# A Taylor attention layer and six windowed-attention layers in one kernel: head norms from a quarter of the array with roots by way of DRAM, queries packed for two groups, the final norm in three places

## The chip, the cores and the metric

The kernel runs on one core of a Trainium2 chip. The metric is the device time of one execution in microseconds (us). A core has five engines that run side by side, each with its own queue of instructions taken in order: TensorE (PE in the profile; its weight loads are listed apart as PEld), VectorE (DVE), ScalarE (ACT), GpSimd (POOL) and SyncE (SP), which here only issues DMAs. An instruction waits at the head of its engine's queue until the semaphores that it needs are set, and everything behind it on that engine waits too.

## The reference

Eight sequences (B = 8) of 512 tokens (N) with 128 features go through two residual blocks. The first is an attention whose weights are a second-order Taylor polynomial of the scores, with a root-mean-square norm of every head's output:

```python
q, k = heads of 16 features;  v = heads of 64           # 16 heads
A = tril(1 + s + s*s/2),  s = q . k / 4                 # qf . kf of taylor_exp
y = A @ v
y = y * rsqrt(mean(y*y over the 64) + 1e-5) * g_weight
out = y @ Wo.T
x = x + layernorm(out)                                  # of layernorm(x) as the input
```

The second block is a stack of six layers, each a local attention in windows of 32 with rotary tables and a gated feed-forward part:

```python
for i in range(6):
    x = attn_layer(shift_tokens(x), ...) + x
    x = ffn_layer(shift_tokens(x), ...) + x
x = x_before + layernorm(x)
```

All is in float32.

## The kernel before

**Two stages.** In the first, the Taylor attention runs over 8 sequences times 4 groups of 4 heads: 32 groups (G = 4b + g). In the second, the six layers run over 6 x 8 x 4 units of 128 tokens (t = 0 to 191), as one software pipeline in which the steps of a unit are spread over later units (`at(t, lag, step)`). The order of TensorE's instructions is the order of the program (`manual_schedule` for PE). On the other engines a scheduler sets the order ahead of time, from priorities and its own idea of durations; `high_priority` and `issue_behind` steer it.

**Tiles.** Pools hand out tiles by tag, and a tag has one to three buffers. A new tile of a tag waits until the last readers of the tile that held its buffer are done. PSUM has four tags: `mm` (2 buffers of 2 banks), `tr` (2 of 1 bank), and `s` (1 of 2 banks). Tags are shared between the stages, so that `t2`, for one, holds roots of head norms in the first stage and half of the turned q and k in the second.

**The first stage** is a list of slots, three to a group: `slot(k)` with k = 3G + ph. In a slot, `squares(k)` multiplies k and q of the group in four row tiles of 32 rows (L261) for the blocks of 128 keys in `STEPS`, ScalarE squares the sums (L270), and VectorE adds one and applies the triangle to the diagonal block (L274). Two slots later `weigh` multiplies with v in two column tiles of 64 columns (L291) into y (PSUM tag `s`, one buffer). After a group's last step, in the next group's slot ph 1, VectorE copies y out with the sums of earlier blocks added (yT, L299, high priority) and ScalarE squares it (ysq, L304). `head_norm(G - 2)` stands in slot ph 0 of every group. It multiplies the squares with a 128x128 block matrix of ones (`same`), so that every feature's row receives its head's sum (L312, two matmuls over 512 columns, two passes each in float32), takes Ln (L313) and Exp (L315) on ScalarE for the roots, and multiplies y by gain and root on VectorE (L317). Between them, `project_qk` (L230, L231) makes q and k of the next group in ph 1, `project_v` (L239, L243) its v in ph 2.

For each sequence, `attn_out(b - 1)` stands in group 1's slot ph 2 of the next sequence: 32 output matmuls over the four groups of the sequence (L327), a layer norm (L335), the residual on GpSimd (L336), a store of 256 KB to DRAM (L337, `x1`) and a second layer norm (L340). `to_state(b - 1)` transposes that into the stack's state three slots later. The next sequence's input is loaded (L145), normed (L200) and transposed (`in_by_features`) in groups 0 and 1.

After the last slot the second stage begins; its unit t = 0 holds `head_norm(31)`, its unit t = 1 `attn_out(7)`.

**The second stage**, for one unit: `proj` (L430, then L438, L446, L454, and L461 on GpSimd), `values` (L488), `sum_squares`, `unit_length` (L474, L477 on GpSimd), `by_features` (transposes, L69), `scores` (L551, maxima L559, exponentials L563), `by_keys`, `weigh_values` (L592), `out_by_features`, `out_project` (L621); for a whole sequence, every fourth unit, `feed_norm`, `feed_first`, `feed_middle` (L646, L648) and `feed_last` (L681). In the units with gelus (every fourth), ScalarE loads the Gelu table and then the table of Ln and Exp again. In the last layer, nine units behind, `out_by_tokens` transposes the result (L699) and `store` norms it (L709: statistics L106 and L108, root L95 and L97, L118 on VectorE), adds the residual on GpSimd (L712) and stores it (L713). Both stand in a unit with gelus.

**At the start**, SyncE issues the first weights (`tw[:, 0]`), the first input, and the other weights in that order.

Of the kernel before, what the change touches and what calls it, by code (L numbers as in the profile page):

```python
# [8 lines left out]
F32 = mybir.dt.float32  # L9
# [19 lines left out]
def sandwich_kernel(ctx: ExitStack, tc: tile.TileContext, ins: dict, out: bass.AP):  # L29
# [20 lines left out]

    dram = ctx.enter_context(tc.tile_pool(name="dram", bufs=1, space=bass.MemoryType.DRAM))
    x1 = [dram.tile([P, NB, DM], F32, tag=f"x1_{b}", name=f"x1_{b}") for b in range(B)]
    state = [const.tile([P, N + 1], F32, tag=f"state_{b}", name=f"state_{b}") for b in range(B)]
    for b in range(B):
        nc.vector.memset(state[b][HD:P, 0:1], 0.0)
# [37 lines left out]
    def inverse_root(dst, src, bias=0.0):  # L93

        ln = nc.scalar.activation(dst, src, AF.Ln, bias=bias)  # L95
        issue_behind(ln, tables[-1])
        exps.append(nc.scalar.activation(dst, dst, AF.Exp, scale=-0.5))  # L97

    def layer_norm(pool, dst, src, nb, by_log=False, later=False):


        st = pool.tile([P, nb, 6], F32, tag="ln_st", name="ln_st")
        mv = pool.tile([P, nb, 2], F32, tag="ln_mv", name="ln_mv")
        rs = pool.tile([P, nb], F32, tag="ln_rs", name="ln_rs")
        for j in range(nb):
            nc.vector.bn_stats(st[:, j, :], src[:, j, :])  # L106
        for j in range(nb):
            nc.vector.bn_aggr(mv[:, j, :], st[:, j, :])  # L108
        if by_log:
            inverse_root(rs, mv[:, :, 1], eps)  # L110
        else:
            nc.vector.tensor_scalar(rs, mv[:, :, 1], EPS, None, ALU.add)
            nc.scalar.activation(rs, rs, AF.Sqrt)
            nc.vector.reciprocal(rs, rs)

        def last(behind=None):
            for j in range(nb):
                t = nc.vector.tensor_scalar(  # L118
                    dst[:, j, :], src[:, j, :], mv[:, j, 0:1], rs[:, j : j + 1], ALU.subtract, ALU.mult
                )  # L120
                if behind is not None:
                    issue_behind(t, behind)

        if later:
            return last
        last()
# [4 lines left out]
    f2 = ctx.enter_context(tc.tile_pool(name="f2", bufs=2))  # L131
    f3 = ctx.enter_context(tc.tile_pool(name="f3", bufs=3))
    f1 = ctx.enter_context(tc.tile_pool(name="f1", bufs=1))

    HF = HD // 2
    NP = H // 2
# [30 lines left out]
    nc.vector.memset(same, 0.0)  # L167
# [56 lines left out]

    def project_qk(G):
        b, g = divmod(G, NQ)
        gr[G]["qk"] = qk = f2.tile([P, 2, N], F32, tag="pe", name=f"tqk_{G}")
        for s in range(2):
            ps = psum.tile([P, N], F32, tag="tr", name="qk")
            nc.tensor.matmul(ps, wqk[:, s, g * P : (g + 1) * P], bt[b]["xlT"], start=True, stop=True)  # L230
            nc.scalar.copy(qk[:, s], ps)  # L231

    def project_v(G):
        b, g = divmod(G, NQ)
# [16 lines left out]
    def squares(k):  # L251

        G, s = steps[k]
        qk = gr[G]["qk"]
        sc = [psum.tile([P, 2, N], F32, tag="mm", name="sc") for _ in range(2)]
        at_, places = 0, []
        for m in STEPS[s]:
            n = N - m * P
            for h in range(4):
                r = slice(32 * h, 32 * h + 32)  # L260
                nc.tensor.matmul(  # L261
                    sc[h // 2][:, h % 2, at_ : at_ + n],
                    qk[r, 1, m * P : (m + 1) * P], qk[r, 0, m * P :], start=True, stop=True,
                    skip_group_check=True,
                )
            places.append((m, at_, n))
            at_ += n
        am = f2.tile([P, 4, 512], F32, tag=("qk", "v2")[k % 2], name="am")
        for i in range(2):
            nc.scalar.activation(  # L270
                am[:, 2 * i : 2 * i + 2, :at_], sc[i][:, :, :at_], AF.Square, bias=1.0, scale=0.25
            )
        for m, o, n in places:
            nc.vector.scalar_tensor_tensor(  # L274
                am[:, :, o : o + P], am[:, :, o : o + P], 1.0,
                keep.unsqueeze(1).to_broadcast([P, 4, P]), ALU.add, ALU.mult,
            )
        gr[G]["am", s] = am, places

    def weigh(k):  # L280
# [12 lines left out]
                    start=(m == 0), stop=(m == NB - 1), skip_group_check=True,  # L293
                )
        if s == len(STEPS) - 1:
            yT = f2.tile([P, 2, NB, P], F32, tag="sq", name="yT")
            with tc.high_priority():
                for i in range(2):
                    nc.vector.tensor_tensor(  # L299
                        yT[:, i], y[:, i].rearrange("p (n m) -> p n m", m=P),  # L300
                        bt[b]["vs"][:, 2 * g + i, :].unsqueeze(2).to_broadcast([P, NB, P]), ALU.add,
                    )
            ysq = f2.tile([P, 2, N], F32, tag="t1", name="ysq")
            nc.scalar.activation(ysq, yT.rearrange("p a n m -> p a (n m)"), AF.Square)  # L304
            gr[G]["yT"], gr[G]["ysq"] = yT, ysq

    def head_norm(G):
        yT, ysq = gr[G].pop("yT"), gr[G].pop("ysq")
        rs = f2.tile([P, 2, N], F32, tag="t2", name="rs")
        for i in range(2):  # L310
            ps = psum.tile([P, N], F32, tag="tr", name="ms")
            nc.tensor.matmul(ps, same, ysq[:, i], start=True, stop=True)  # L312
            ln = nc.scalar.activation(rs[:, i], ps, AF.Ln, bias=eps4, scale=1.0 / HD)  # L313
            issue_behind(ln, tables[-1])
        exps.append(nc.scalar.activation(rs, rs, AF.Exp, scale=-0.5))  # L315
        gr[G]["yn"] = yn = f1.tile([P, 2, N], F32, tag=("qT", "pT", "on", "oT")[G % NQ], name="yn")
        nc.vector.scalar_tensor_tensor(  # L317
            yn.rearrange("p a n -> p (a n)"), yT.rearrange("p a n m -> p (a n m)"), gw,
            rs.rearrange("p a n -> p (a n)"), ALU.mult, ALU.mult,
        )  # L320

    def attn_out(b):

# [28 lines left out]
    def slot(k):  # L352
# [2 lines left out]
        b, g = divmod(G, NQ)  # L355
        if k < len(steps):
            squares(k)
        if ph == 0 and 0 <= G - 2 < NG:
            head_norm(G - 2)
        if ph == 1 and G + 1 < NG:  # L360
            project_qk(G + 1)
        if ph == 2 and G + 1 < NG:
# [4 lines left out]
            in_by_features(b + 1)  # L367
        if g == 1 and ph == 1 and b + 1 < B:
            sums_before(b + 1)
        if g == 1 and ph == 2 and b >= 1 and k < len(steps):  # L370
            attn_out(b - 1)
        if g == 2 and ph == 2 and b >= 1 and k < len(steps):
            to_state(b - 1)
        if 0 <= k - 2 < len(steps):
            weigh(k - 2)
# [326 lines left out]
            u["out"] = fo = f1.tile([P, NB, DM], F32, tag="fo", name="fo")  # L702
            nc.scalar.copy(fo, ps)

    def store(u):

        b, src = u["b"], u["out"]
        fo = src if b < B - 1 else f1.tile([P, NB, DM], F32, tag="fo", name="fo")
        layer_norm(f2, fo, src, NB, by_log=True)  # L709
# [19 lines left out]
    with tc.manual_schedule(engines={mybir.EngineType.PE}):  # L729
# [8 lines left out]
        for t in range(len(units) + 7):  # L738
# [49 lines left out]
            at(t, 1, scores)  # L788
            if t == len(units) + 5:
                at(t, 6, out_by_tokens)  # L790
                at(t, 6, store)
            at(t, 3, feed_normed, ends=True)
            at(t, 2, out_by_features)

# [37 lines left out]

def _attn_weights(given):

    import numpy as np

    parts = []
    for nm in ("Wq", "Wk"):
        w = given[f"L0_attn_{nm}"].reshape(H, FD, DM)
        parts.append(np.pad(w, ((0, 0), (0, FD), (0, 0))).reshape(2 * FD * H, DM).T)  # L840
    parts.append(given["L0_attn_Wv"].T)
    parts.append(given["L0_attn_Wo"].T.reshape(H // 2, P, DM).transpose(1, 0, 2).reshape(P, H // 2 * DM))
    return np.ascontiguousarray(np.concatenate(parts, 1))


# [39 lines left out]
```

## Time and profile before

| what | value |
|---|---|
| median of three runs | 3693.85 us (3693.65 to 3706.11) |
| the profiled execution | 3691.65 us |
| its span | 3689.8 us |
| granted TensorE clock, mean | 0.995 |
| first matmul of the first slot to the last y matmul of the first stage | 17.94 to about 532.24 us |
| six sequences' periods in the first stage, from L327 to L327 | 65.61, 67.25, 65.67, 65.67, 67.25, 62.03 us |
| four units in the fifth layer and at the start of the sixth | 64.35 us |
| four units with a store | 67.14 to 67.23 us |

The span runs from the first to the last instruction that the profiler shows. The granted clock is 0.97 in every third slice of 50 us and 1.00 in the others, which is where the periods of 67.25 us lie. Times of float32 matmuls come in pairs of passes: an instruction of the program is two instructions in the profile. Neighbouring matmuls overlap a little, so that what one step takes on TensorE is read from its start to the start of the next step, and is a little less than the duration beside it.

### The profile page before, as it was taken

The numbers are of one execution on the slowest core, as the hardware profiler recorded it, in microseconds if no ns is written. First come the engines' busy times: TensorE is split into PE (matmuls) and PEld (weight loads), VectorE is DVE, ScalarE is ACT, GpSimd is POOL, SyncE is SP. The second block draws the span as 40 slices with busy tenths as digits, with TensorE's granted clock in tenths as the row PEclk, the third lists the DMA queues.
The fourth block names the chain that finished last, engine by engine and source line by source line (L and its number), as shares of the span: only waits on it lengthen the run. The fifth ranks groups of instructions, "written<-read, shape, count | busy, mean of one in ns | idle before, by whom it ended". The sixth has DMA issues, their size and how long they took to land.

```text
span 3689.8 us, 152840 instructions
## 1 busy us (share of the span) xinstructions
PE 3632.2 (98%) x65216; PEld 2421.6 (66%) x65216; DVE 2808.2 (76%) x3915; ACT 2825.4 (77%) x6944; POOL 1844.7 (50%) x1311
## 2 busy tenths in 40 slices
PE   8999999999999999999999999999999999999997
PEld 4555556666676766667676666767666766766665
DVE  4555557788787878788787878878887887888885
ACT  5565557878787888888788888878888887877875
POOL 0000016555565555656555656656555565655552
PEclk9999999999999999999999999999999999999998
DMA  3000003222232222322222322222322222222221
GB/s 85 18 10 7 12 18 92 68 61 69 66 93 66 68 67 66 83 76 70 63 66 66 92 74 60 69 67 78 78 71 68 60 68 68 67 66 71 70 74 43
DMA packets 153220, 233.67 MB, mean 63 GB/s; under 512 B 32622, under 2 KB 53356, under 8 KB 151788
## 3 DMA queue, kind: packets, MB, share of 16 engines
q1 hardware_dynamic: 152556, 223.89, 23.7%
q8 instruction: 530, 8.68, 1.0%
q14 instruction: 134, 1.10, 0.1%
HBM read 24.54 MB, written 4.19 MB: 8 GB/s over the span
## 4 chain that ended last, share of the span: by engine, by line
PE 90%; ACT 8%; DVE 1%; issue 1%; POOL 0%; DMA 0%; POOLq 0%; DVEq 0%; SPq 0%; ACTq 0%
PE tr L69 19%; PE mm L430 14%; PE py L621 9%; PE mm L488 9%; PE po L592 8%; PE sp L551 6%; PE y L291 4%; ACT pe L563 4%; PE mm L646 4%; PE mm L648 3%; PE py L681 3%; PE sc L261 3%; PE vv L239 2%; PE po L327 1%; PE qk L230 1%; ACT L75 1%
## 5 line engine op out<-in xcount | busy, mean ns | idle before, releaser
L461 POOL TENSOR_TENSOR qk<-t,t 128x1024 f32<-128x1024 f32 x384 | 910.6, 2372 | 622.7 <-DVE t L446 414.6
L477 POOL TENSOR_TENSOR qk<-qk,ss 128x1024 f32<-128x1024 f32 x384 | 723.2, 1905 | 16.0
L430 PE MATMUL mm<-wqkv,state 128*128 128x512 f32 x1536 | 700.2, 596 | 2.6 <-ACT v L493 2.6
L563 ACT ACTIVATE pe<-sp,mx 128x64 f32<-128x64 f32 x3072 | 654.3, 381 | 7.6 <-DVE mx L559 7.6
L438 DVE TENSOR_TENSOR t<-mm,tab 128x1024 f32<-128x1024 f32 x384 | 468.2, 1219 | 217.5 <-PE mm L430 214.5
L454 ACT ACTIVATE sq<-mm 128x512 f32<-128x512 f32 x768 | 420.2, 603 | 126.9 <-DVE t L446 124.5
L446 DVE TENSOR_TENSOR t<-mm,tab 128x1024 f32<-128x1024 f32 x384 | 468.2, 1219 | 7.3 <-POOL qk L461 1.4
L430 PEld LDWEIGHTS mm<-wqkv,state 128*128 128x128 f32 x1536 | 273.0, 190 | 292.0 <-issue 240.9
L464 DVE TENSOR_REDUCE ss<-sq 128x16 f32<-128x1024 f32 x384 | 448.7, 1209 | 0.1
L69 PE MATMUL tr<-ident,qk 128*128 128x128 f32 x3072 | 441.8, 277 | 1.8 <-POOL qk L461 0.8
L69 PEld LDWEIGHTS tr<-ident,qk 128*128 128x128 f32 x3072 | 351.7, 141 | 120.1 <-issue 56.1
L621 PE MATMUL py<-oT,wo 128*128 128x128 f32 x3072 | 377.3, 276 | 0.3 <-ACT oT L614 0.3
L621 PEld LDWEIGHTS py<-oT,wo 128*128 128x128 f32 x3072 | 367.6, 195 | 0.5 <-ACT oT L614 0.5
L488 PE MATMUL mm<-wqkv,state 128*128 128x512 f32 x768 | 361.5, 593 | 0.2 <-ACT sq L454 0.2
L614 ACT COPY oT<-tr 128x512 f32<-128x512 f32 x384 | 205.5, 587 | 168.3 <-PE tr L69 165.7
L551 PEld LDWEIGHTS sp<-kT,qT 64*32 64x32 f32 x24576 | 264.4, 105 | 92.8 <-issue 55.3
L592 PE MATMUL po<-v,pT 64*32 64x64 f32 x24576 | 296.9, 226 | 9.6 <-issue 6.1
L551 PE MATMUL sp<-kT,qT 64*32 64x64 f32 x24576 | 298.2, 225 | 1.2 <-issue 1.2
L592 PEld LDWEIGHTS po<-v,pT 64*32 64x32 f32 x24576 | 269.0, 105 | 46.3 <-issue 22.6
L527 ACT COPY qT<-tr 128x512 f32<-128x512 f32 x384 | 226.2, 589 | 94.0 <-PE tr L69 93.0
L474 POOL TENSOR_SCALAR ss<-ss 128x32 f32<-128x32 f32 x192 | 55.1, 287 | 480.4 <-ACT ss L97 433.0
L527 ACT COPY kT<-tr 128x512 f32<-128x512 f32 x384 | 225.9, 588 | 73.4 <-PE tr L69 73.0
(109 smaller groups left out, 5392.1 us busy)
## 6 DMA issues: line engine op xcount, KB each, us to landing
v<-v SPq DMA_DIRECT2D x1152, 128.0 KB
v<-v SPq DMA_DIRECT2D x672, 64.0 KB
wqkv<-in_L_ffn_Wqkv_dram SPq DMA_DIRECT2D x6, 1536.0 KB
wo<-in_L_ffn_Wo_dram SPq DMA_DIRECT2D x6, 512.0 KB
xin<-_attn_hidden_states_dram SPq DMA_DIRECT2D x8, 256.0 KB
xr<-_attn_hidden_states_dram SPq DMA_DIRECT2D x8, 256.0 KB
x<-xr SPq DMA_DIRECT2D x8, 256.0 KB
xr<-x SPq DMA_DIRECT2D x8, 256.0 KB
```

What stands on the lines that cost most here:

```text
L69: nc.tensor.transpose(ps[:cols, :rows], src, ident[:rows, :rows])
L430: nc.tensor.matmul(ps[:, a].rearrange("p h d -> p (h d)"), lhs, wqkv[:, s, a, :], start=True, stop=True)
L438: nc.vector.tensor_tensor(t2, ps[:, ::-1], tab[:, 2 * s + 1, j, :].rearrange("p (a d) -> p a d", a=2).unsqueeze(2) .to_broadcast([P, 2, H, ...
L446: nc.vector.tensor_tensor(t1, ps, tab[:, 2 * s, j, :].rearrange("p (a d) -> p a d", a=2).unsqueeze(2) .to_broadcast([P, 2, H, HF]), ALU.mult,)
L461: nc.gpsimd.tensor_tensor(qk[:, s].rearrange("p h a d -> p a h d"), t1, t2, ALU.add)
L477: nc.gpsimd.tensor_tensor(t, t, ss[:, i, :].unsqueeze(2).to_broadcast([P, H, HD]), ALU.mult)
L488: nc.tensor.matmul(ps[:, p, :], lhs, L["wqkv"][:, 2, p, :], start=True, stop=True)
L527: copies.append(nc.scalar.copy(dst, ps))
L551: nc.tensor.matmul(sp[W * w : W * (w + 1), p, pair, :], qT[HD * p : HD * (p + 1), pair, W * w : W * (w + 1)], kT[HD * p : HD * (p + 1), pa ...
L563: ex = nc.scalar.activation(pe[:, pair, p, :], sp[:, p, pair, :], AF.Exp, bias=mx[:, p, pair : pair + 1])
L592: nc.tensor.matmul(po[W * w : W * (w + 1), p, pair, :], pT[r, pair, W * w : W * (w + 1)], v2[r, w, HD * pair : HD * (pair + 1)], start=(pa ...
L621: nc.tensor.matmul(py, L["wo"][:, c, :], oT[:, c, :], start=(c == 0), stop=(c == NP - 1))
```

## The change

**The head norm** now takes two groups at a time. `of` has 32 columns, with ones in every second column for the first 64 rows and in the others for the last 64. Four matmuls, one for each half of each group's squares, write 32 partitions each of one PSUM tile. Two rows of every quarter then differ, the sums of two heads. One Ln and one Exp over 128x512 give the roots, four DMAs of two rows (2 KB each) write them to a tile in DRAM (`roots`, two of them in turn), and four DMAs read them back, each to 64 partitions (256 KB). `rt` shares the tag `gT` (one buffer) with `ao` of `attn_out`; the tiles `rs` keep the tag `t2`. VectorE multiplies in place. `head_norm(G - 3)` stands in slot ph 0 of every odd group, for the groups G - 3 and G - 2; the last pair is in unit t = 0. `yT` has six places in turn.

**Queries** of two groups are packed: q has 16 features of an even group's head and 16 of the next group's in the same 32 rows, and k has zeros in the other group's 16 rows. q is projected in even groups only. The order of the heads in the weights of v and of the output follows on the host.

**attn_out and to_state** are moved: `attn_out(b - 1)` from group 1, ph 2, to group 2, ph 0, and `to_state(b - 1)` from group 2, ph 2, to group 3, ph 0.

**The norm of the final result** is in three parts: statistics (`out_stats`) nine units behind, root (`out_roots`) and the rest (`store`) ten units behind, the latter issued on VectorE behind that unit's maxima. For the last sequence all three follow each other as before.

**The first input** is loaded ahead of the first weights.

```diff
@@ layer_norm
+        if later == "roots":
+            return lambda: inverse_root(rs, mv[:, :, 1], eps), last
@@ load order
+    load_x(0)
     nc.sync.dma_start(tw[:, 0], a_w[:, 0])
-    load_x(0)
@@
-    same = const.tile([P, P], F32, tag="same", name="same")
-        nc.vector.memset(same[HD * a : HD * (a + 1), HD * a : HD * (a + 1)], 1.0)
+    of = const.tile([P, W], F32, tag="of", name="of")
+        nc.vector.memset(of[HD * a : HD * (a + 1), a::2], 1.0)
@@ project_qk
-        gr[G]["qk"] = qk = f2.tile([P, 2, N], F32, tag="pe", name=f"tqk_{G}")
-        for s in range(2):
+        k = f2.tile([P, 2, N], F32, tag="pe", name=f"tk_{G}")[:, 0]
+        q = fq.tile([P, N], F32, tag="tq", name=f"tq_{G}") if g % 2 == 0 else gr[G - 1]["q"]
+        gr[G]["q"], gr[G]["k"] = q, k
+        for s, dst in ((0, q), (1, k))[g % 2 :]:
+            cols = slice(g * P, (g + 1) * P) if s else slice(g // 2 * P, (g // 2 + 1) * P)
...
@@ weigh
-            yT = f2.tile([P, 2, NB, P], F32, tag="sq", name="yT")
+            i = (G + 2) % (NQ + 2)
+            yT = (f1 if i < NQ else f2).tile(
+                [P, 2, NB, P], F32, tag=("qT", "pT", "on", "oT", "sq", "sq")[i], name="yT"
+            )
@@ head_norm
-        rs = f2.tile([P, 2, N], F32, tag="t2", name="rs")
-        for i in range(2):
-            ps = psum.tile([P, N], F32, tag="tr", name="ms")
-            nc.tensor.matmul(ps, same, ysq[:, i], start=True, stop=True)
-            ln = nc.scalar.activation(rs[:, i], ps, AF.Ln, bias=eps4, scale=1.0 / HD)
-            issue_behind(ln, tables[-1])
-        exps.append(nc.scalar.activation(rs, rs, AF.Exp, scale=-0.5))
-        gr[G]["yn"] = yn = f1.tile([P, 2, N], F32, tag=("qT", "pT", "on", "oT")[G % NQ], name="yn")
-        nc.vector.scalar_tensor_tensor(
-            yn.rearrange("p a n -> p (a n)"), yT.rearrange("p a n m -> p (a n m)"), gw,
-            rs.rearrange("p a n -> p (a n)"), ALU.mult, ALU.mult,
-        )
+        ps = psum.tile([P, N], F32, tag="tr", name="ms")
+        for c in range(4):
+            nc.tensor.matmul(
+                ps[W * c : W * (c + 1)], of, gr[G + c // 2]["ysq"][:, c % 2], start=True, stop=True,
+                skip_group_check=True,
+            )
+        rt = f1.tile([P, NCH, N], F32, tag="gT", name="rt")[:, 0]
+        ln = nc.scalar.activation(rt, ps, AF.Ln, bias=eps4, scale=1.0 / HD)
+        issue_behind(ln, tables[-1])
+        exps.append(nc.scalar.activation(rt, rt, AF.Exp, scale=-0.5))
+        rd = roots[G // 2 % 2]
+        for c in range(4):
+            nc.sync.dma_start(rd[c // 2, :, c % 2], rt[W * c : W * c + 2])
+        for g in range(2):
+            rs = f2.tile([P, 2, N], F32, tag="t2", name="rs")
+            for a in range(2):
+                nc.sync.dma_start(rs[HD * a : HD * (a + 1)], rd[g, a].partition_broadcast(HD))
+            yT = gr[G + g]["yT"].rearrange("p a n m -> p (a n m)")
+            nc.vector.scalar_tensor_tensor(yT, yT, gw, rs.rearrange("p a n -> p (a n)"), ALU.mult, ALU.mult)
@@ slot
-        if ph == 0 and 0 <= G - 2 < NG:
-            head_norm(G - 2)
+        if ph == 0 and G % 2 and 0 <= G - 3 < NG:
+            head_norm(G - 3)
-        if g == 1 and ph == 2 and b >= 1 and k < len(steps):
+        if g == 2 and ph == 0 and b >= 1 and k < len(steps):
             attn_out(b - 1)
-        if g == 2 and ph == 2 and b >= 1 and k < len(steps):
+        if g == 3 and ph == 0 and b >= 1 and k < len(steps):
             to_state(b - 1)
@@ the units
-                head_norm(NG - 1)
+                head_norm(NG - 2)
...
+            after = 10 + NB * B * (DEPTH - 1) <= t < len(units) + 6
+            if after:
+                at(t, 10, out_roots, ends=True)
             if ends:
                 at(t, 9, out_by_tokens, ends=True)
+                at(t, 9, out_stats, ends=True)
             at(t, 5, feed_middle, ends=True)
-            if ends:
-                at(t, 9, store, ends=True)
             at(t, 6, feed_last, ends=True)
             at(t, 1, scores)
+            if after:
+                at(t, 10, store, ends=True)
```

More of the change, by code (lines that the diff above doesn't have):

```diff
@@ L52, in sandwich_kernel @@
     x1 = [dram.tile([P, NB, DM], F32, tag=f"x1_{b}", name=f"x1_{b}") for b in range(B)]
+    roots = [dram.tile([2, 2, 2, N], F32, tag=f"roots_{i}", name=f"roots_{i}") for i in range(2)]
     state = [const.tile([P, N + 1], F32, tag=f"state_{b}", name=f"state_{b}") for b in range(B)]
@@ L108, in layer_norm @@
             nc.vector.bn_aggr(mv[:, j, :], st[:, j, :])
[L109 to L114, printed above, removed]
         def last(behind=None):
@@ L122, in last @@
                     issue_behind(t, behind)
+        if later == "roots":
+            return lambda: inverse_root(rs, mv[:, :, 1], eps), last
+        if by_log:
+            inverse_root(rs, mv[:, :, 1], eps)
+        else:
+            nc.vector.tensor_scalar(rs, mv[:, :, 1], EPS, None, ALU.add)
+            nc.scalar.activation(rs, rs, AF.Sqrt)
+            nc.vector.reciprocal(rs, rs)
         if later:
@@ L133, in sandwich_kernel @@
     f1 = ctx.enter_context(tc.tile_pool(name="f1", bufs=1))
+    fq = ctx.enter_context(tc.tile_pool(name="fq", bufs=2))
     HF = HD // 2
@@ L164, in sandwich_kernel @@
     )
-    same = const.tile([P, P], F32, tag="same", name="same")
-    nc.vector.memset(same, 0.0)
+    of = const.tile([P, W], F32, tag="of", name="of")
+    nc.vector.memset(of, 0.0)
     for a in range(2):
-        nc.vector.memset(same[HD * a : HD * (a + 1), HD * a : HD * (a + 1)], 1.0)
+        nc.vector.memset(of[HD * a : HD * (a + 1), a::2], 1.0)
     eps4 = const.tile([P, 1], F32, tag="eps4", name="eps4")
@@ L226, in project_qk @@
         b, g = divmod(G, NQ)
-        gr[G]["qk"] = qk = f2.tile([P, 2, N], F32, tag="pe", name=f"tqk_{G}")
-        for s in range(2):
+        k = f2.tile([P, 2, N], F32, tag="pe", name=f"tk_{G}")[:, 0]
[3 more added lines that the diff above has]
+            cols = slice(g * P, (g + 1) * P) if s else slice(g // 2 * P, (g // 2 + 1) * P)
             ps = psum.tile([P, N], F32, tag="tr", name="qk")
-            nc.tensor.matmul(ps, wqk[:, s, g * P : (g + 1) * P], bt[b]["xlT"], start=True, stop=True)
-            nc.scalar.copy(qk[:, s], ps)
+            nc.tensor.matmul(ps, wqk[:, s, cols], bt[b]["xlT"], start=True, stop=True)
+            nc.scalar.copy(dst, ps)
     def project_v(G):
@@ L253, in squares @@
         G, s = steps[k]
-        qk = gr[G]["qk"]
+        tq, tk = gr[G]["q"], gr[G]["k"]
         sc = [psum.tile([P, 2, N], F32, tag="mm", name="sc") for _ in range(2)]
@@ L262, in squares @@
                     sc[h // 2][:, h % 2, at_ : at_ + n],
-                    qk[r, 1, m * P : (m + 1) * P], qk[r, 0, m * P :], start=True, stop=True,
+                    tk[r, m * P : (m + 1) * P], tq[r, m * P :], start=True, stop=True,
                     skip_group_check=True,
@@ L307, in head_norm @@
     def head_norm(G):
[L308 to L320 removed]
+        ps = psum.tile([P, N], F32, tag="tr", name="ms")
[17 more added lines that the diff above has]
+            nc.vector.scalar_tensor_tensor(yT, yT, gw, rs.rearrange("p a n -> p (a n)"), ALU.mult, ALU.mult)
+            gr[G + g]["yn"] = gr[G + g]["yT"].rearrange("p a n m -> p a (n m)")
     def attn_out(b):
@@ L703, in out_by_tokens, with out_stats, out_roots, store @@
             nc.scalar.copy(fo, ps)
[L705 to L709, printed above, removed]
+    def out_stats(u):
+        u["fo"] = fo = u["out"] if u["b"] < B - 1 else f1.tile([P, NB, DM], F32, tag="fo", name="fo")
+        u["roots"], u["normed"] = layer_norm(f2, fo, u["out"], NB, later="roots")
+    def out_roots(u):
+        u.pop("roots")()
+    def store(u, behind=True):
+        b, fo = u["b"], u["fo"]
+        u.pop("normed")(maxima[-1] if behind else None)
         xr = f1.tile([P, NB, DM], F32, tag="xr", name="xr")
@@ L784, in sandwich_kernel @@
                 at(t, 0, unit_length)
-            if ends:
-                at(t, 9, store, ends=True)
             at(t, 6, feed_last, ends=True)
             at(t, 1, scores)
+            if after:
+                at(t, 10, store, ends=True)
             if t == len(units) + 5:
                 at(t, 6, out_by_tokens)
-                at(t, 6, store)
+                at(t, 6, out_stats)
+                at(t, 6, out_roots)
+                at(t, 6, store, False)
             at(t, 3, feed_normed, ends=True)
@@ L835, in _attn_weights @@
     import numpy as np
[L837 to L842, printed above, removed]
+    heads = [8 * (g // 2) + 2 * r + g % 2 for g in range(H // 4) for r in range(4)]
+    wq = given["L0_attn_Wq"]
+    wk = given["L0_attn_Wk"].reshape(H, FD, DM)
+    k = np.zeros((H // 4, 4, 2, FD, DM), wk.dtype)
+    for i, h in enumerate(heads):
+        k[i // 4, i % 4, i // 4 % 2] = wk[h]
+    wv = given["L0_attn_Wv"].reshape(H, HD, DM)[heads].reshape(H * HD, DM)
+    wo = given["L0_attn_Wo"].T.reshape(H, HD, DM)[heads]
+    parts = [
+        np.pad(wq, ((0, FD * H), (0, 0))).T,
+        k.reshape(2 * FD * H, DM).T,
+        wv.T,
+        wo.reshape(H // 2, P, DM).transpose(1, 0, 2).reshape(P, H // 2 * DM),
+    ]
     return np.ascontiguousarray(np.concatenate(parts, 1))
```

## The prediction

> **What bounds the kernel now.** I read the page first.
>
> ```profile
> PE 3632.2 (98%) x65216; PEld 2421.6 (66%) x65216; DVE 2808.2 (76%) x3915; ACT 2825.4 (77%) x6944; POOL 1844.7 (50%) x1311
> ```
>
> TensorE is nearly always busy, and the chain that ended last gives it 90%. So a step is worth what it takes off TensorE in its own stage, plus the waits of TensorE that it removes, minus those that it makes. Second, the timeline of TensorE in one sequence's period, first stage (start, length, instructions):
>
> ```profile
> 239.36 1.94 PE L291 MATMUL y<-am,tv 128*64 128x512 f32 x8
> 241.23 1.14 PE L261 MATMUL sc<-tqk 32*128 32x512 f32 x8
> 242.30 1.98 PE L312 MATMUL ms<-ysq,same 128*128 128x512 f32 x4
> 244.21 1.51 PE L291 MATMUL y<-am,tv 128*64 128x384 f32 x8
> 245.65 1.75 PE L261 MATMUL sc<-tqk 32*128 32x384 f32 x8
> 247.34 1.98 PE L230 MATMUL qk<-xlT,tw 128*128 128x512 f32 x4
> 249.25 1.52 PE L291 MATMUL y<-am,tv 128*64 128x256 f32 x16
> ...
> 286.55 0.66 PE L69 MATMUL tr<-ident,xl 128*128 128x128 f32 x4 [0.69 <-ACT rs L313]
> ```
>
> No gaps: from start to start, L312 takes 1.91 us and L230 (q and k) 1.91. Two places per sequence are stretched by ScalarE: L261 of 384 columns (1.69 where it takes 0.87 elsewhere) and 0.69 ahead of the transposes. Third, what ScalarE and VectorE spend on it (busy us, mean ns, idle):
>
> ```profile
> L270 ACT ACTIVATE am<-sc 128x768 f32<-128x768 f32 (+1 forms) x192 | 158.9, 874 | 66.8 <-PE sc L261 66.3
> L317 DVE SCALAR_TENSOR_TENSOR yn<-yT,vec,rs 128x1024 f32<-128x1024 f32 x32 | 42.1, 1317 | 29.8 <-ACT rs L315 29.7
> L313 ACT ACTIVATE rs<-ms,eps 128x512 f32<-128x512 f32 x64 | 41.2, 693 | 2.2 <-POOL qk L461 1.4 <-PE ms L312 0.9
> L315 ACT ACTIVATE rs<-rs 128x1024 f32<-128x1024 f32 x32 | 33.8, 1057 | 0.7
> ```
>
> Fourth, the chain of waits at the join of the stages, and fifth, VectorE in a unit of the last layer that holds a store:
>
> ```profile
> 522.03 1.52 ACT am L270 x2
> ...
> 524.28 1.30 DVE yT L299 x2
> 525.58 0.14 issue
> 525.72 1.94 PE y L291 x8
> ```
>
> ```profile
> 3308.23 0.60 DVE L118 TENSOR_SCALAR fo<-fo,ln_mv,ln_rs 128x128 f32<-128x128 f32 x2 [1.22 <-ACT ln_rs L97]
> 3308.75 1.22 DVE L559 TENSOR_REDUCE mx<-sp 128x16 f32<-128x1024 f32 x1
> 3309.89 2.65 DVE L118 TENSOR_SCALAR fo<-fo,ln_mv,ln_rs 128x128 f32<-128x128 f32 x2
> 3312.46 1.21 DVE L438 TENSOR_TENSOR t<-mm,tab 128x1024 f32<-128x1024 f32 x1
> ```
>
> Here the norm's last step delays the maxima by 0.6 us and the next unit's L438 by 2.65 (two that elsewhere take 0.7; GpSimd's L477 runs until 3312.45). Such four units take 67.14 us and not 64.35.
>
> **Sums of squares: -43.5 us.** Before, 32 groups x 1.91 = 61.1. After, 16 pairs with eight passes over 512 columns in four column tiles. Eight full passes (L430) take 3.63, eight in two column tiles 1.87 (first row above), eight in four row tiles 1.07. I take 1.1, by the last: 17.6. Bounds: 0.91 (3.63 / 4) and 3.63 (no overlap), so -46.5 to -3.0.
>
> [...] In the trace L291's loads (137 ns, same rows) add nothing: 1.87 against 3.63 / 2. [...]
>
> **Queries: -15.3.** 16 of 64 projections go, 0.955 each. k's zeros change no size.
>
> **ScalarE: -10.6.** Per pair 2 x (2 x 0.693 + 1.057) = 4.89 become 0.693 and half of 1.057 plus overhead, about 1.3; 16 copies of 0.59 go too. ScalarE waits 66.3 us for L261 as it is, so 66 us less work counts only where TensorE waited for it: the two places above, 0.82 + 0.69, in seven sequences. The moved `attn_out` now hides the first behind 7.3 us of L327, and the sums take one `tr` buffer, not two, which frees the transposes. Bounds 0 and -10.6.
>
> **New waits in the slots: +16.** (a) L261 needs both halves of ScalarE's last squares (2 x 1.03 us). In group 0 nothing stands between but y over 384 columns (1.44), where L312 gave 1.91 more: about 0.6 x 8 = 4.8. (b) `attn_out` is moved ahead of y in group 2. In the changed order of ScalarE the root of the second norm stands ahead of ysq and of the next squares; it waits for statistics, GpSimd's sum (1.27) and statistics again, about 5.9 us from L327's end. ysq then ends at 9.5 and both squares at 11.3, where TensorE wants the PSUM at 9.4 to 10: 1.6 x 7 = 11.2. Bounds 0 and double, 32.
>
> **The way by DRAM: 0.** Eight DMAs per pair, 128 in all, on SyncE's queue. Count from the end of the sums, T. ScalarE is squaring until T + 1.0; Ln and Exp end at T + 2.3. Four writes issue in 4 x 0.34 (as L337), and land within 1.8 (mean wait for L337's store; longest 2.3). Reads start near T + 5, and two issue in 0.9. No row shows such a read alone. Bounds: 1.8, and 9.3, the only broadcast (issued at 3.72, consumed at 13.02, among the first loads). I take 3, nearer to the plain transfer since the queues are 95% idle there: the first root tile is there at T + 8.5, the second 1.2 later.
>
> ```profile
> SPq L332 <- DMA x<-xr: 12.4, 7, 2.3
> ```
>
> Behind the waiting multiply on VectorE stand the copy of v (L243) and the triangle, never yT of that slot, which the changed order puts ahead. What TensorE wants of these first: in group 1 the `tr` buffer for L327, 13.9 us after T by the rows above; in group 3 the one for L230, 14.2. With 1.3 for the multiply and 0.7 for the copy, roots that land by T + 12 cost nothing. At the upper bound, T + 14.5, each pair costs 2.5, 40 in all. On SyncE the roots of the group-3 pair stand behind the moved store and the load after it, which waits for the second norm; that load issues some 9 us after L327, Exp ends near 14: no wait.
>
> **The join: +3.5.** There the cover is gone. The last multiply pair stands ahead of the last group's triangle (L274), so that y waits until T + 11.0 for what it would have at 9: 2 us. Then the last roots must go by DRAM after GpSimd's L461 frees `t2`, and `attn_out(7)` wants the product: L327's seventh matmul is 4 us late, of which the waits for GpSimd and ScalarE that stand there now give back more than half: 1.5 us. Bounds 0 and 8.
>
> **The start: -1.2.** The first input was waited for until 5.48; 512 KB less stands ahead of it. But L230 then needs the weights. Bounds 0 and -2.
>
> **The last layer: -10.** Four units cost 2.8 more with a store; 0.44 are transposes, which stay. The rest, 2.35, is the multiply in the gelu unit. A unit later VectorE is idle for 1.5 us behind the maxima (waiting for L430), and L118 takes 4 x 0.34 and perhaps 0.7 behind GpSimd. I take 0.45 left: 1.9 x 5 periods, and 0.5 in the drain. Bounds -14 and 0.
>
> **Sum**, against the profiled execution: 3691.65 - 43.5 - 15.3 - 10.6 + 16 + 3.5 - 1.2 - 10 = 3630.6. The median is 2.2 above that execution, and I forecast the median: 3632.
>
> **Rivals.**
> - *The read is as slow as the first broadcast*: 40 us more, and a late join: 3672 to 3680. For it: many engines reading the same 4 KB, and it is the only row. Against it: that row lay under 3 MB of other loads.
> - *Column tiles by four do not overlap*: 40.5 more, 3673. Against it L291.
> - *The last step of the final norm hits GpSimd again*, ScalarE's relief comes to nothing: 10 + 10 more, 3652. Inside the range.
> - *Slower*: VectorE stands at the multiply for a round trip that is longer than any row here, in all 16 pairs, with v's copy and all else behind it. The gain of 61 is spent at 3.8 us per pair, roots at T + 15.8; slower by 0.5% from T + 17.0, that is 15 us after Exp where I count 6. At T + 18 it is 3632 + 96 = 3728. Against it: the highest sum of rows stays below 13.
>
> **How the numbers follow.** A run of this kernel can tell about 0.5%, 18.5 us. Forecast with its terms between their bounds, 3612 to 3652: 0.76. Slow read or no overlap, 3655 to 3680: 0.14. Slower: 0.04. Below 3612: 0.04. The rest, 0.02, no change. The range 3612 to 3664 takes in the first and a third of the second, 0.81. Faster by over 0.5% is below 3675: forecast, below, and most of the second case: 0.92; no change 0.04, slower 0.04.
>
> **What would show it.** L312's successor should take 1.0 to 1.2 us per pair and start to start sequences some 59 us; L230 96 passes. VectorE's multiply should wait for DMA, but TensorE not for v or `tr`; L261 should be stretched in groups 0 and 2. Four units with a store should take 64.8 to 65.5. I am wrong if TensorE shows gaps behind the multiply, or 3 us for the sums.

## The result and the profile after

The changed kernel takes 3640.26 us (median of four runs, 3638.86 to 3643.02), the kernel before 3693.98 in the same comparison: ratio 0.9853, 95% interval 0.984 to 0.9866. The profiled execution took 3643.02, the longest of the four, its span 3641.2 us, at a mean granted clock of 0.993 (before 0.995). The page's first part:

```profile
PE 3575.2 (98%) x65184; PEld 2404.3 (66%) x65184; DVE 2796.4 (77%) x3915; ACT 2765.6 (76%) x6864; POOL 1843.6 (51%) x1311
```

TensorE lost 57 us of work and is as full as before. The timeline of TensorE, in one sequence's period of the first stage, shows what took the place of the lines shown of before:

```profile
229.45 1.94 PE L299 MATMUL y<-am,tv 128*64 128x512 f32 x8 [0.80 <-DVE yT L311]
231.32 1.66 PE L269 MATMUL sc<-tq,tk 32*128 32x512 f32 x8
232.90 1.06 PE L324 MATMUL ms<-ysq,of 128*32 128x512 f32 x8
233.90 0.66 PE L70 MATMUL tr<-ident,xs 128*128 128x128 f32 x4
...
245.88 1.51 PE L299 MATMUL y<-am,tv 128*64 128x384 f32 x8
247.31 1.57 PE L269 MATMUL sc<-tq,tk 32*128 32x384 f32 x8
248.81 1.13 PE L238 MATMUL qk<-xlT,tw 128*128 128x512 f32 x2
```

Eight passes in four column tiles take 1.00 us from start to start (232.90 to 233.90), once per pair of groups, where L312 took 1.91 per group. L238 takes 1.06 where q rides along from the group before. Two new waits are there, where the prediction put them: y stands 0.80 behind VectorE and the next L269 is stretched by 0.5 (group 2); L269 over 384 columns is stretched by 0.63 (group 0). The old ones are gone: the transposes of xl follow L324 at once. The 0.80 comes from VectorE, which works at the second norm (L107, L112) before it copies y out (L311), 2.2 us after the last matmul of y; ScalarE's ysq waits 1.94 for the same copy:

```profile
225.67 0.87 DVE L107 BATCH_NORM_STATS2 ln_st<-xr 128x6 f32<-128x128 f32 x4 [1.44 <-POOL xr L357]
...
227.52 0.59 DVE L112 TENSOR_SCALAR xs<-xr,ln_mv,ln_rs 128x128 f32<-128x128 f32 x2
228.02 1.28 DVE L311 TENSOR_TENSOR yT<-y,vs 128x512 f32<-128x512 f32 x2
```

The groups of ScalarE and VectorE that answer to those shown before (busy us, mean ns, idle before them):

```profile
L278 ACT ACTIVATE am<-sc 128x768 f32<-128x768 f32 (+1 forms) x192 | 158.4, 875 | 73.4 <-PE sc L269 73.3
L340 DVE SCALAR_TENSOR_TENSOR yT<-yT,vec,rs 128x1024 f32<-128x1024 f32 x32 | 42.5, 1327 | 14.3 <-DMA rs<-roots 14.3
L329 ACT ACTIVATE rt<-ms,eps 128x512 f32<-128x512 f32 x16 | 11.1, 691 | 2.3 <-PE ms L324 2.3
L331 ACT ACTIVATE rt<-rt 128x512 f32<-128x512 f32 x16 | 10.3, 641 | 0.3
```

The multiply waits for the DMA, 14.3 us in all, 3.7 of them at the join, and in the slots TensorE waits for it once, 0.52 us (L348 at 448.53). VectorE in a unit of the last layer that holds a store:

```profile
3286.94 1.23 DVE L580 TENSOR_REDUCE mx<-sp 128x16 f32<-128x1024 f32 x1
3288.20 1.51 DVE L112 TENSOR_SCALAR fo<-fo,ln_mv,ln_rs 128x128 f32<-128x128 f32 x4
3289.68 1.22 DVE L459 TENSOR_TENSOR t<-mm,tab 128x1024 f32<-128x1024 f32 x1
```

The norm's last step now stands behind the maxima and takes 1.51, in the gap where VectorE had nothing; four such units take 64.90 to 64.96.

The join of the stages went otherwise. TensorE there, in the timeline of the changed kernel:

```profile
491.48 1.05 PE L348 MATMUL po<-tw,yT 128*128 128x128 f32 x8
495.10 1.22 PE L348 MATMUL po<-tw,yT 128*128 128x128 f32 x4 [2.56 <-DVE yT L340]
498.78 7.52 PE L348 MATMUL po<-tw,yT 128*128 128x128 f32 x52 [2.46 <-DVE yT L340]
...
521.47 1.22 PE L613 MATMUL po<-v,pT 64*32 64x64 f32 x102
524.59 0.43 PE L613 MATMUL po<-v,pT 64*32 64x64 f32 x26 [1.90 <-issue]
...
560.65 3.60 PE L451 MATMUL mm<-wqkv,state 128*128 128x512 f32 x8
568.19 1.94 PE L70 MATMUL tr<-ident,pe 128*128 128x128 f32 x8 [3.94 <-issue]
569.92 3.62 PE L642 MATMUL py<-oT,wo 128*128 128x128 f32 x16
```

Two waits for the multiply stand inside the output product. On VectorE the first multiply waits 3.70 for its roots, and two products of unit 1 stand between it and the second, which starts 5.2 us behind:

```profile
492.25 2.79 DVE L340 SCALAR_TENSOR_TENSOR yT<-yT,vec,rs 128x1024 f32<-128x1024 f32 x1 [3.70 <-DMA rs<-roots]
...
497.45 1.27 DVE L340 SCALAR_TENSOR_TENSOR yT<-yT,vec,rs 128x1024 f32<-128x1024 f32 x1
```

Then come pauses for which the profile names no engine and no transfer ("issue"). Behind the longest one, at unit 5, eight transposes take 1.94 us and sixteen matmuls 3.62, where 1.07 and 1.95 are usual.

| stretch, in the profiled executions | before | after | difference |
|---|---|---|---|
| start to the first L269 | 17.94 | 16.04 | -1.9 |
| to the first projection L451 | 514.30 | 462.92 | -51.4 |
| to the first projection at the steady pace (unit 7) | 103.01 | 118.39 | +15.4 |
| layers 1 to 5 | | | +0.8 |
| last layer | | | -11.5 |
| span | 3689.8 | 3641.2 | -48.6 |

The third row is the measure of the join below: from the first projection to the first one that takes 3.79 us, which every kernel has in unit 7.

### The profile page after: what moved, and what is told of

The parts are those of the page before. It is cut to its first block, busy times and chain, and to the rows that moved or that the text cites. A ratio compares the mean times of both kernels' runs of the same rounds, so it can differ in the third digit from the quotient of the medians.

```text
span 3641.2 us, 153034 instructions
## 1 busy us (share of the span) xinstructions
PE 3575.2 (98%) x65184; PEld 2404.3 (66%) x65184; DVE 2796.4 (77%) x3915; ACT 2765.6 (76%) x6864; POOL 1843.6 (51%) x1311
## 4 chain that ended last, share of the span: by engine, by line
PE 87%; ACT 9%; DVE 2%; issue 1%; DMA 1%; POOL 0%; SPq 0%; POOLq 0%; DVEq 0%; ACTq 0%
PE tr L70 19%; PE mm L451 14%; PE py L642 10%; PE mm L509 9%; PE po L613 8%; PE sp L572 6%; ACT pe L584 4%; PE mm L667 4%; PE mm L669 4%; PE y L299 3%; PE py L702 3%; PE sc L269 2%; PE po L348 2%; ACT L76 1%; PE vv L247 1%; ACT oT L635 1%
## 5 line engine op out<-in xcount | busy, mean ns | idle before, releaser
L451 PE MATMUL mm<-wqkv,state 128*128 128x512 f32 x1536 | 700.3, 596 | 0.6 <-issue 0.6
L451 PEld LDWEIGHTS mm<-wqkv,state 128*128 128x128 f32 x1536 | 273.1, 190 | 289.8 <-issue 242.4
L70 PE MATMUL tr<-ident,qk 128*128 128x128 f32 x3072 | 440.9, 276 | 1.8 <-ACT qT L548 0.8
L70 PEld LDWEIGHTS tr<-ident,qk 128*128 128x128 f32 x3072 | 351.3, 141 | 120.7 <-issue 56.3
```

The costliest lines, as they stand in the source:

```text
L70: nc.tensor.transpose(ps[:cols, :rows], src, ident[:rows, :rows])
L451: nc.tensor.matmul(ps[:, a].rearrange("p h d -> p (h d)"), lhs, wqkv[:, s, a, :], start=True, stop=True)
```

## The experiments

**Padding at unit 5.** Where the repeating schedule begins (unit 5), both kernels align TensorE's instructions: `addr_align(128, offset=IN_STEP)` fills up with instructions that do nothing until the next one stands at place 98 of 128. Before that point the change has fewer instructions, so that the run of padding has another length. By a count of the built program, which no trace holds, 2335 places lie between the output product of the last sequence and unit 5, so that a second alignment ahead of that product sets the length. The numbers of padding instructions are worked out in this way; how many the unaltered kernels have is not known.

```diff
             if t == 1:
+                nc.tensor.addr_align(128, offset=61)
                 attn_out(B - 1)
```

> The changed kernel with one more alignment of TensorE's instructions, set where it waits for the last roots anyway, so that about 6 padding instructions are left at the first unit of the repeating schedule (unit 5). Theory (the pause of 3.4 us there and the half clock after it come from the number of padding instructions): the pause falls below 0.5 us, the stretch of 10 us after it runs at full clock, and the time falls from 3640 to 3630-3634 us. Rival (the DMAs of the roots, or the shorter first stage itself, starve the instruction supply): pause and clock stay, 3638-3642 us.

With `offset=77`:

> The same with about 118 padding instructions left at unit 5. Theory: a pause of 3.5-7 us there, the clock dip after it, 3640-3646 us; 9 us or more above the run with few. Rival: no different from the run with few, both at 3638-3642 us.

The kernel before with `offset=9`:

> The kernel before, nothing else of the change in it, with an alignment in the same place that leaves about 58 padding instructions at unit 5. Theory: it gets the pause of about 3.4 us and the clock dip that only the changed kernel showed, and is 4-9 us slower than before: 3698-3703 us. Rival (it needs the roots' DMAs): as before, 3692-3696 us.

And the kernel before with `addr_align(128, offset=4)` as TensorE's first instruction, ahead of `in_by_features(0)`:

> The kernel before, with an alignment of TensorE's instructions as its very first (where TensorE waits for the input), placed so that about 121 padding instructions stand at unit 5. Theory (the pause belongs to a long run of padding, whatever kernel it is in): a pause of 4-5 us at that place, then transposes and matmuls at about half speed, and 3699-3704 us against 3693. Rival (a long run is only harmful behind the changed kernel's join, with the roots' DMAs shortly before): 3692-3695 us.

| kernel | median us | ratio to before | pause at unit 5 | the join |
|---|---|---|---|---|
| changed | 3640.26 | 0.9853 [0.984, 0.9866] | 3.9 | 118.4 |
| changed, about 6 | 3633.55 | 0.9839 [0.9822, 0.9855] | none | 107.1 |
| changed, about 118 | 3638.96 | 0.9855 [0.984, 0.9869] | 4.75 | 115.4 |
| before | 3693.42 | 1 | none | 103.0 |
| before, about 58 | 3693.28 | 0.9999 [0.999, 1.0008] | none | 102.4 |
| before, about 121 | 3700.68 | 1.0021 [1.0012, 1.0031] | 5.1 | 107.7 |

The intervals are those of each run's own comparison; the last row's has the kernel before at 3692.67, so that it lost 8.0. For about 118 the forecast was 3640 to 3646 us and at least 9 above the run with few: the pause came as forecast, the time is 5.4 above.

TensorE at unit 5, with about 6 in the changed kernel:

```profile
558.48 3.60 PE L451 MATMUL mm<-wqkv,state 128*128 128x512 f32 x8
561.91 1.06 PE L70 MATMUL tr<-ident,pe 128*128 128x128 f32 x8
562.81 1.95 PE L642 MATMUL py<-oT,wo 128*128 128x128 f32 x16
```

with about 118:

```profile
567.76 1.94 PE L70 MATMUL tr<-ident,pe 128*128 128x128 f32 x8 [4.75 <-issue]
569.49 3.62 PE L642 MATMUL py<-oT,wo 128*128 128x128 f32 x16
```

and with about 121 in the kernel before:

```profile
615.03 1.94 PE L69 MATMUL tr<-ident,pe 128*128 128x128 f32 x8 [5.11 <-issue]
616.76 2.40 PE L621 MATMUL py<-oT,wo 128*128 128x128 f32 x16
```

So the pause, and the slow stretch behind it, belong to a long run of padding, also in a kernel that has no roots in DRAM: the rival falls. It isn't a price per instruction: about 58 cost nothing, which the third expectation missed, and about 120 cost 5 us and a slow stretch. One rival is left. The padding ends at a fixed place, so that its length and the place where it begins change together, and no run tells one from the other. The added alignment shows in the trace as well: a pause of 4.56 us (few) or 5.35 (118) ahead of the output product, hidden in part behind the wait for the multiply. From the first projection to the product's end it is 27.7 and 29.9 us, in the changed kernel 27.3. The clock in the windows around the pause (us, each engine's busy us and instructions, then the granted clock, DMA share and GB/s), first of the changed kernel, then of the one with about 6:

```profile
564.00:574.00 10.00, 6.06 (x31) 5.84 (x31) 3.66 (x5) 2.93 (x8) 2.82 (x2) 0.66 0.20 53
```

```profile
562.00:572.00 10.00, 9.96 (x306) 8.30 (x305) 8.87 (x11) 8.04 (x17) 5.44 (x4) 1.00 0.23 59
```

What makes TensorE pause is not shown; what the runs show at unit 5 is a pause of 4.75 us at about 118 and of 5.11 at about 121 instructions that do no work, and none at about 58 or fewer.

Of the 11.3 us by which the joins of the changed kernel and the one with few differ, the pause at unit 5 is 4.1 from start to start and the slow instructions behind it 2.4. Another 2.1 are a second pause behind these (1.97), and 2.6 are pauses of 1.90 and less ahead of unit 5. These last two kinds are missing in the run with about 118, so the long run of padding is not shown to be their cause. The medians differ by 6.7 us only: the profiled execution of the changed kernel was its longest.

**The join without the way by DRAM.** The last pair gets the old matrix of ones back, two sums per group, and writes the roots where `t2` was, as before the change.

```diff
             if t == 0:
-                head_norm(NG - 2)
+                head_norm_ones(NG - 2)
+                head_norm_ones(NG - 1)
...
```

> The changed kernel, its last pair of groups (30, 31) with the old head norm, a matrix of ones and no way by DRAM, and an alignment as TensorE's first instruction that leaves about 9 padding instructions at unit 5. Theory (the 6 us that the join loses before the last output product are the roots' way by DRAM): the product's matmuls no longer wait for VectorE's multiply behind a DMA; y end to the end of the product falls from 27-28 us to 22-24, and the time is 3-6 us below the run with few padding instructions (3633.5): 3628-3631 us. Rival (those 6 us are GpSimd's sum and the buffers t2, as before the change): within 1.5 us of 3633.5.

3636.77 us (ratio 0.9847 [0.9832, 0.9862]): not faster, above both forecasts. The alignment, here TensorE's first instruction, delays the first transposes from 5.96 to 8.53 us; but the first projection to the product's end took 28.6 us against 27.7. The timeline of TensorE tells why:

```profile
490.07 3.78 PE L328 MATMUL ms<-ysq,same 128*128 128x512 f32 x4 [4.53 <-ACT rs L329]
...
502.68 6.07 PE L365 MATMUL po<-tw,yT 128*128 128x128 f32 x52 [1.11 <-DVE yT L333]
```

The sums of the second group wait for ScalarE, which may not write roots into `t2` until GpSimd's sum has read the projections' products. The rival named that buffer. So next only the buffers and the order are changed, and the way by DRAM stays:

```diff
-            rs = f2.tile([P, 2, N], F32, tag="t2", name="rs")
+            rs = f2.tile([P, 2, N], F32, tag="pe" if G == NG - 2 else "t2", name="rs")
...
+            if u is units[1]:
+                issue_behind(tt, mults[-1])
```

> The changed kernel with few padding instructions (about 8) at unit 5, and the last pair's roots read into tiles of their own, not into the two t2 buffers that the projections' products share; the products of unit 1 stand behind both multiplies on VectorE. Theory (the join's 6 us before the output product's end are those buffers and the order on VectorE, not the way by DRAM): the second multiply starts within 1.5 us of the first one's start, not 5; the product's last 52 matmuls start some 3 us earlier; y end to the end of the product 24 us where it was 27-28; 3628.5-3631.5 us against 3633.5. Rival (the second root tile lands too late, or GpSimd stretches the multiplies as before): within 1.5 us of 3633.5.

3630.41 us (ratio 0.983 [0.9814, 0.9847]), the join 105.1. VectorE:

```profile
493.27 1.30 DVE L341 SCALAR_TENSOR_TENSOR yT<-yT,vec,rs 128x1024 f32<-128x1024 f32 x1 [0.64 <-DMA rs<-roots]
495.68 1.73 DVE L341 SCALAR_TENSOR_TENSOR yT<-yT,vec,rs 128x1024 f32<-128x1024 f32 x1 [1.11 <-DMA rs<-roots]
```

The two multiplies start 2.4 us apart, not 5.2, where 1.5 was expected; the second is now bound by its transfer. From the first projection to the product's end it is 25.95 us, 1.8 less, where 24 was expected: the second root tile itself lands that late. The median lies where the theory had it, 3.1 below the kernel with few, but the two intervals overlap, and the profiled executions differ by 1.0 only, with the same delay at the start in the way: it is the trace that speaks for the theory, not the time.

**The length of the trip.** `roots` is copied twice more from DRAM to DRAM before it is read.

```diff
+        for to in hop[G // 2 % 2]:
+            nc.sync.dma_start(to, rd)
+            rd = to
```

> The changed kernel (about 6 padding instructions at unit 5) with two more transfers from DRAM to DRAM between the roots' writes and their reads, each about 2.7 us by the writes' issue and landing. Theory (the prediction's account: roots that land by 12 us after the sums cost nothing, each us after that costs one us in each of 16 pairs): the second root tile lands 14-15 us after the sums, 2-3 us of each pair are lost, 3633.5 + 32 to 48 + 4 at the join = 3670-3686 us. Rival (VectorE's wait stays off TensorE's path, only the join pays): 3636-3643 us.

3682.36 us (ratio 0.9971 [0.996, 0.9983]): 48.8 above the kernel with few padding instructions, 39 of it in the first stage and 12.6 at the join. The reads are issued 6.2 us after the writes, not 1.6. The waits of TensorE (total us, times, longest):

```profile
PE po L352 <- DVE yT L344: 27.8, 16, 2.9
```

The size was as the prediction's account had it, the way to it was not, so that the agreement is in part luck. VectorE stands waiting for these transfers in 4 places only (9.6 us): the built order puts the multiply some 17 us behind the sums, behind other work of VectorE. What pays is the output product, which starts 14 us behind the sums of the pair of groups 2 and 3; it waits 3.3 us in each of seven sequences, 23 of the 39 us. The rest comes with slow stretches: the granted clock is 0.95 to 0.98 in the windows of 100 us from 100 to 500, in the kernel with few 0.98 to 1.00 from 100 to 400, and sequences take 62.4 to 65.6 us where 58.5 was the rule. A trip that is 4.6 us longer leaves 10 us of the gain, less than the final norm alone is worth.

**One part alone.** The kernel before with only the final norm in three places, and with only the packed q (and an alignment at the start, for few padding instructions):

```diff
...
-        layer_norm(f2, fo, src, NB, by_log=True)
...
+        u["roots"], u["normed"] = layer_norm(f2, fo, u["out"], NB, later="roots")
```

> The kernel before with only the norm of the final result taken apart in three places. Theory (the last layer's five stores each give back about 2.3 us, whatever the first stage does): 3681-3684.5 us, 9.5-12.5 below before, and the units with a store at 64.9 us. Rival (part of that came from the other edits, for example from a join that leaves the engines in other places): less than 6 us, 3688 us or more.

```diff
+        for s, dst in ((0, q), (1, k))[g % 2 :]:
+            cols = slice(g * P, (g + 1) * P) if s else slice(g // 2 * P, (g // 2 + 1) * P)
...
```

> The kernel before with q packed for two groups alone (and an alignment as TensorE's first instruction that leaves few padding instructions at unit 5). Theory (16 projections of 0.955 us off TensorE's path, and 16 copies off ScalarE, which matter only where TensorE waits for it): -15 to -20, 3673-3679 us. Rival (the projections filled time in which TensorE waits for ScalarE's squares, so that waits take their place): less than 8 us, 3685 us or more.

The norm alone: 3680.88 us, ratio 0.9968 [0.9956, 0.998], 12.5 less, units with a store 64.86 to 65.00. Its rival falls. The packed q alone: 3681.17, ratio 0.9968 [0.9957, 0.998], 11.5 less, between the two forecasts. TensorE there:

```profile
271.58 1.13 PE L234 MATMUL qk<-xlT,tw 128*128 128x512 f32 x2
272.64 1.52 PE L295 MATMUL y<-am,tv 128*64 128x256 f32 x16
...
311.45 1.49 PE L265 MATMUL sc<-tq,tk 32*128 32x256 f32 x16
```

A projection less is 0.85 us less (1.06 where the pair takes 1.91), so 13.6 in all; and once in each sequence L265 is now stretched by 0.55 behind ScalarE, and the sums wait 0.26. Sequences take 64.8, not 65.67: eight times 0.87 is 7 of the 11.5 us. The trace of before also has two periods of 67.25, each with one slice of 50 us at a clock of 0.97 (from 200 and from 400; the others from 50 to 500 are at 1.00: every fourth slice there, not every third), and this one has none like them; what is left is not assigned. The rest of the change (the head norm, the moved steps, the start) is then worth about 36 us with few padding instructions (59.9 - 12.5 - 11.5), if the parts add up; it was not run alone.

**The two new waits.** The second norm goes behind y of its phase, and in group 0 the next keys are projected a phase earlier.

```diff
-        if ph == 1 and G + 1 < NG:
+        if ph == (0 if g == 0 else 1) and G + 1 < NG:
             project_qk(G + 1)
...
+        if g == 2 and ph == 1 and b >= 1 and k < len(steps):
+            norm_again(b - 1)
```

> The changed kernel with few padding instructions at unit 5, and two edits in the slots: the second norm behind the output product is computed after the group's y (its statistics behind the addition to yT on VectorE), and in group 0 the next keys are projected one phase earlier, ahead of the triangle products that waited for ScalarE's squares. Theory (the two new waits, 1.3 us in group 2 and 0.63 in group 0, come from the order and leave nothing in their place): sequences of 56.5-57 us start to start, not 58.49; 3619-3623 us. Rival (ScalarE or PSUM bounds the groups, and a wait of like size appears at the next product): sequences of 58 us or more, 3629 us or more.

3624.16 us (ratio 0.9811 [0.9797, 0.9826]), sequences of 57.32: between the two. Both waits are gone, and two fifths of their 1.9 us came back one step on, as the timeline of TensorE shows:

```profile
223.96 1.14 PE L272 MATMUL sc<-tq,tk 32*128 32x512 f32 x8
225.03 1.06 PE L328 MATMUL ms<-ysq,of 128*32 128x512 f32 x8
226.67 0.66 PE L70 MATMUL tr<-ident,xs 128*128 128x128 f32 x4 [0.58 <-DVE tv L254]
...
243.45 1.14 PE L272 MATMUL sc<-tq,tk 32*128 32x256 f32 x16
```

1.3 + 0.63 - 0.58 - 0.2 = 1.15 per sequence, as measured (58.49 to 57.32). The alignment at the start is in this kernel too, and in the next two.

**All in one**, and then with the matrix of ones for the last pair in tiles of its own:

> All of these in one: few padding instructions at unit 5, the last roots in tiles of their own with their multiplies first, the second norm later, the keys of group 1 earlier. Theory (each acts at a place of its own, so they add up): 3633.5 - 3 - 12 = 3616-3620 us. Rival (the join gives back what the slots gain, as the change itself showed): 3626 us or more.

> The kernel with all edits (3621.65), and in it the last pair of groups with a matrix of ones and no way by DRAM, its roots in tiles of their own and its multiplies first on VectorE. Theory (with the buffers out of the way, what the join still loses is the way by DRAM, some 8 us from the last sums to the first product): TensorE has no wait for VectorE's multiply over 0.5 us, the first projection to the end of the output product takes 21-23 us, not 26-27.5, in spite of 3 us more of sums, and the median is 3616-3619. Rival (the remainder is the half clock behind the pauses, or the projections' own products on VectorE): 25 us or more, and 3621-3624.

3621.65 us (0.9809 [0.9794, 0.9823]) and 3622.11 (0.9804 [0.9791, 0.9818]). Both beat the kernel before and the changed one, and neither is to be told from the kernel with the two waits alone, nor from the other. The first lies just above its forecast of 3616 to 3620, the second where its rival put it (3621 to 3624). The first one's profiled execution (3629) had pauses of "issue" again, one of 2.29 behind a slow stretch. In the second no wait for the multiply is left:

```profile
485.43 3.70 PE L481 MATMUL mm<-wqkv,state 128*128 128x512 f32 x8 [2.32 <-DVE ss L519]
488.96 7.31 PE L372 MATMUL po<-tw,yT 128*128 128x128 f32 x64
```

From the first projection to the product's end it takes 23.4 us, as without the change plus the sums (21.1 + 1.9), and yet the join is 104.6, 0.5 less than with the roots by DRAM in tiles of their own: what comes earlier there waits for ScalarE two units on (1.50 at L70). So at the join the way by DRAM costs 2.5 us up to the product, and no difference in the time could be measured.

## Why the prediction was right

The time was 3640.26 where 3632 was forecast, inside the range; the mechanism and most sizes held, one term was far off, and some agreements are luck.

- *Sums of squares* (1.1 per pair): 1.00. Column tiles by four overlap like row tiles (1.07). Their weight loads, eight of 108 ns in the changed trace, did not come on top: that would have made it 1.9.
- *Queries* (-15.3): 13.6 by the rows, 11.5 alone; 0.955 was half of the pair's 1.91, but a projection that stands alone takes 1.06, and ScalarE took some back.
- *ScalarE* (-10.6): the two old waits, 1.51 per sequence, are gone, as forecast.
- *New waits* (+16): group 2 cost 1.3 (forecast 1.6), group 0 0.63 (0.6). That they came from the order, the run with two edits showed: there both are gone. In group 2 the place was right and the engine half right: 0.8 of the 1.3 is VectorE's copy of y standing behind the second norm, where the prediction named only ScalarE.
- *The four terms together*, per sequence: four sums of 1.91 became two of 1.00 (-5.64), two projections (-1.70), the old waits (-1.51), the new ones (+1.93), in all -6.9; measured were 65.67 to 58.49, -7.2. For the stretch from the first L269 to the first projection the forecast is a loss of 51.4 (53.4, and 2.0 back from the join's term, y behind the last multiply), and 51.4 were measured. That this agrees to a tenth is luck. The 2.0 came to 0.3: the end of y takes 4.91 us to the projection, before 6.52 with a sum of 1.91 in it. With the sizes measured, 31 sums of 1.91 against 15 of 1.00, the stretch would have lost 54.0; the 2.6 between are not assigned.
- *The way by DRAM* (0): a wait of 0.52 us in the slots, once. Where the multiply waits for them, the first roots are there 8.1 to 9.0 us behind the sums, once 10.5 (8.5 forecast), by two errors that cancel: the reads are issued at 3.3 to 4.3 us and not at 5, and from the first issue to the multiply it takes 4.7 to 5.1 us, once 6.2, and not 3.5. The price of a longer trip was tried: two hops, 4.6 us, cost 49. The rival that was slower had the right order of price, by another way than VectorE standing at the multiply in every pair.
- *The last layer* (-10): 2.27 x 5 = 11.3 (units of 67.17 and 64.90), and 12.5 alone.
- *The start* (-1.2): -1.9.
- *The join* (+3.5) is the term that was mis-sized. The 1.5 of it that lay behind the first projection became 15.4, and TensorE shows the gaps behind the multiply that the prediction had named as a sign of being wrong, though, but for the 0.52 us, only there. With few padding instructions it is 4.1, inside the bounds of 0 and 8 and 2.6 more than taken; 2.0 of it went with the buffers and the order on VectorE, by which the second multiply came 5.2 us behind the first. The 11.3 on top (6.7 by the medians) are pauses and slow stretches of TensorE. 6.5 of them, the pause at unit 5 and the slow instructions behind it, go with a run of padding whose length the change shifted, in a line that the diff does not touch; for the other pauses no cause is shown. The sum had no term for any of this, and the trace of before shows no such pause at unit 5.

What stays open: at how many padding instructions the pause begins (between 58 and 118), whether the length or the place of the padding counts, why TensorE pauses there at all, and 2.4 us that the kernel before with about 121 lost after unit 7.

## What to carry to other kernels

Where a program aligns its instructions by padding, count what an edit ahead of it does to the padding, and put the long runs where the engine waits anyway. At the very start an alignment left the first transposes of the kernel before at 7.76 us (7.75 without), but moved them to 9.45 with the packed q, and in the changed kernel from 5.96 to 8.53. Where a stage ends, nothing covers a round trip, and a shared buffer or another engine's order can cost as much as the trip itself (2.0 and 2.5 us here): change these first. A wait that is ordered away comes back in part at the next product; three fifths of it were gained here.

## What was not expected of the hardware

About 58 padding instructions cost nothing, about 120 stopped TensorE for 4.75 to 5.1 us, and the granted clock over the 10 us of pause and slow stretch was 0.66 in the changed kernel, where eight transposes took 1.94 us and not 1.07; the kernel before with about 121 had 0.86 over 12 us. Runs of one kernel spread over 3 to 6 us here, twice over more than 11, and four profiles hold pauses of 1.9 to 2.3 us without a releaser, three of them of their kernel's longest execution. Not every such pause belongs to padding: the trace of before has five of 1.23 us at L592 in the last layer, and they are gone with the norm in three places.
